# Earlier stream starts, a pause before layer 3, and one transpose for the R rows in a four-layer graph attention kernel

## The chip, the cores and the metric

The kernel runs on one core of one Trainium2 chip. The metric is the device time of one execution in microseconds; the number to beat is the median of three runs.

## What is computed

The input is x of 32 batches, 512 nodes, 256 features, and one 512 x 512 adjacency matrix shared by all batches. Four pre-norm layers follow each other; each adds its output to x. The first three are graph attention layers on relu(layernorm(x)): a projection, two scores per node, a leaky relu of their sum, a softmax over the neighbours, a weighted sum. Layer 2 does this with four heads of 64 features. Layer 3 is a linear layer to 512 features, an attention over all nodes, a linear layer back to 256, and a masked attention.

```python
def _gat(inp, adj_mask, W, a):
    h = jnp.matmul(inp, W)
    f1 = jnp.matmul(h, a[:F_, 0])
    f2 = jnp.matmul(h, a[F_:, 0])
    e = leaky_relu(f1[:, :, None] + f2[:, None, :], ALPHA)
    if adj_mask is not None:
        e = jnp.where(adj_mask[None, :, :] > 0, e, NEG_INF)
    att = jax.nn.softmax(e, axis=2)
    return elu(jnp.einsum('bij,bjf->bif', att, h))
```

## The kernel before

A batch has four tiles of 128 nodes (NT = 4). Everything is float32, so a matmul is two passes on TensorE (15273 records for some 9300 matmuls and transposes); a transpose is one.

**Attention.** exp(leaky_relu(s + r)) is written as a maximum of two products, so the weight of a pair of nodes is max(R of one, T of the other) times the mask. `values` (L301) projects a tile, takes the exponents of the scores on ScalarE (L312, L315) and scales the values (ScalarE L313 in layer 0, VectorE L316 in layer 1; in layer 2, ScalarE L439 and VectorE L440). `weights` (L336) needs R as a row on all 128 partitions. It gets it in one of two ways. Either four broadcast transposes write it into a PSUM bank (L342), or, for heads 1 to 3 of layer 2, it is sent through DRAM: R of all heads is transposed to rows (L460, four transposes of 4 columns), copied to SBUF (L462), written to `row_d` (L464), and read back once per head onto all partitions as `spread` (L468). Then VectorE makes the weights (L346), and `aggregate` (L358) multiplies them with the values.

**Layer 3.** `linear_t` is the first linear layer (tile WM1), `project_half` projects to 512 features in two halves (WFC). For all batches but the last, the unmasked attention is done by sorting (`sort_attend`, L550): indirect DMAs on GpSimd scatter the rows by rank (L594), SP reads them back (L601, L602), VectorE and TensorE make running sums (L612 to L633, tiles `sums` and `tot`), SP writes them to a table (L634, L635), and GpSimd gathers from it (L642). `mlp_in` and a second `linear_t` follow, then the masked attention with WHA, then the store of x (L701).

**Streams and the clock.** Four streams (NS = 4) each work through every fourth batch. A batch is a Python generator that yields the clock value at which its next step may be issued. The loop at the end (L742) always takes the stream with the smallest value, so the order of instructions is set by a clock of the kernel's own, which is arithmetic: `after_us` (L60) adds to the step's own start twice its TensorE cycles over 2400 plus 1.5 times a stated delay. A scheduler below then moves single instructions by a few places. No instruction waits for this clock on the chip; it only orders them. Each engine takes its instructions in the given order. Stream i starts at clock i * LEAD, LEAD = 75; a batch takes 299.4 units, of which layers 0 to 2 take 130.6. The setup of masks and projected weights is a fifth stream from 7.5 on, a step every 4 units. In `turned` (L285) the first half of a layer's input is transposed, then the stream yields `when`, a value handed on from the layer before, and transposes the second half.

**Buffers.** Each stream has two of the eight PSUM banks (`bank`, L74), taken in turn. In SBUF, `w` has 4 buffers, `v` 4, `hT` 3, `xn` 3, `y` and `q` 3 each, `spread` 2, `y4` 1, `x` 5. The SBUF tile for the R rows comes from the `q` pool.

Of the kernel before, what the change touches and what calls it, by code (L numbers as in the profile page):

```python
# [35 lines left out]
def fast(ctx, tc, flag, x, adj, w0, a0, w1, a1, w2, a2, mlp1_w, mlp1_b, mlp2_w, mlp2_b,  # L36
# [10 lines left out]
    LEAD = 75.0  # L47
    SLOW = 1.5
    STRETCH = 2.0

    const = ctx.enter_context(tc.tile_pool(name="const", bufs=1))
    work = ctx.enter_context(tc.tile_pool(name="work", bufs=2))
# [21 lines left out]
    def bank():  # L74
        return psum.tile([P, N], FP, tag=f"b{turn[0]}", name="b", bufs=8 // NS)
# [209 lines left out]
    def turned(xn, when):  # L285

        hT = work.tile([P, KF, N], FP, tag="hT", name="hT", bufs=3)
        turn_pair(xn, hT, 0)
        yield when
        turn_pair(xn, hT, 2)  # L290
        yield after_us(0.6)
        return hT
# [43 lines left out]
    def weights(r_col, t_col, masked=True, r=None):  # L336
# [15 lines left out]
                nc.vector.tensor_scalar(wt[:, j, :], r, t_col(j), None, op0=OP.max)  # L352
        return wt

    def pair(tag="y"):
        return work.tile([P, 2, F], FP, tag=tag, name=tag, bufs=3)

# [6 lines left out]
        nc.vector.reciprocal(r, den)  # L364
        return r

    def plain(hT, w, rs=None):
        v = yield from values(hT, w, rs)
        wt = weights(lambda t: v[:, t, F + 2:F + 3], lambda j: v[:, j, F + 1:F + 2])
        note(v[:, :, F:])  # L370
        yield after_us(3.2)
        return v, wt
# [16 lines left out]
        nc.vector.tensor_tensor(r, q, r, op=OP.add)  # L389

    def layer0(xt, xn, rs, when):
        v, wt = yield from plain((yield from turned(xn, when)), W0)
        xn, rs = new_xn(), small([NT], "rs")
        for t0 in range(0, NT, 2):
            r, q = pair(), pair("q")
            for i in range(2):
                p, rd = averages(v, wt, t0 + i)
                nc.scalar.activation(q[:, i, :], p, AF.Exp, scale=rd)
                nc.scalar.activation(r[:, i, :], p, AF.Relu, scale=rd)
                if i == 0:  # L400
                    yield after_us(0)
            add_elu(xt[:, t0:t0 + 2, :], r, q)
            norm(xt, xn, rs, t0, True)
            last, when = when, after_us(6)
            if t0 == 0:
                yield after_us(0)
        yield last
        return xn, rs, when

    def layer1(xt, xn, rs, when):  # L410
        v, wt = yield from plain((yield from turned(xn, when)), W1, rs)
        xn, rs = new_xn(), small([NT], "rs")
        for t0 in range(0, NT, 2):
            r = pair()
            for i in range(2):
                p, rd = averages(v, wt, t0 + i)
                nc.scalar.activation(r[:, i, :], p, AF.Relu, scale=rd)
                if i == 0:
                    yield after_us(0)
            xr = xt[:, t0:t0 + 2, :]  # L420
            nc.vector.tensor_tensor(xr, xr, r, op=OP.add)  # L421
            norm(xt, xn, rs, t0, True)
            last, when = when, after_us(5)
            if t0 == 0:
                yield after_us(0)
        yield last
        return xn, rs, when

    def layer2(xt, xn, rs, when):
        hT = yield from turned(xn, when)  # L430
        v = work.tile([P, NT, NH, CH], FP, tag="v", name="v2", bufs=4)
        for t in range(NT):
            ps = bank()
            for k in range(KF):
                matmul(
                    ps[:, :NH * CH], hT[:, k, t * P:(t + 1) * P], W2[:, k, :, :], start=(k == 0), stop=(k == KF - 1)
                )
            pv = ps[:, :NH * CH].rearrange("p (h c) -> p h c", c=CH)
            nc.scalar.activation(v[:, t, :, D:], pv[:, :, D:], AF.Exp, scale=rs[:, t:t + 1])  # L439
            nc.vector.scalar_tensor_tensor(  # L440
                v[:, t, :, :D], pv[:, :, :D], rs[:, t:t + 1], v[:, t, :, D:D + 1].to_broadcast([P, NH, D]),
                op0=OP.mult, op1=OP.mult,
            )
            yield after_us(0 if t + 1 < NT else 1)
        ya = work.tile([P, NT, F], FP, tag="y4", name="y4", bufs=1)
        wts = []

        def begin(h):
            wts.append(
                weights(  # L450
                    lambda t: v[:, t, h, D + 2:D + 3], lambda j: v[:, j, h, D + 1:D + 2], r=spread[h] if h else None
                )
            )
            return after_us(3.2)

        p = bank()
        for t in range(NT):
            transpose(p[:NH, t * P:(t + 1) * P], v[:, t, :, D + 2], ident)  # L460
        row = pair("q").rearrange("p a f -> p (a f)")[:NH, :]
        nc.scalar.copy(row, p[:NH, :])  # L462
        row_d = dram.tile([NH, N], FP, tag="row", name="row", bufs=3)
        nc.sync.dma_start(row_d, row)  # L464
        spread = [None]
        for h in range(1, NH):
            r = work.tile([P, N], FP, tag="spread", name="spread", bufs=2)
            nc.sync.dma_start(r, row_d[h, :].partition_broadcast(P))  # L468
            spread.append(r)
        when = begin(0)  # L470
        note(v.rearrange("p t h c -> p (t h) c")[:, :, D:])
        yield after_us(3)
        for h in range(NH):
            last = when
            if h + 1 < NH:
                when = begin(h + 1)
            yield last
            wt = wts[h]
            p = bank()
            for t in range(NT):  # L480
                aggregate(p[:, t * (D + 1):(t + 1) * (D + 1)], wt, t, lambda j: v[:, j, h, :D + 1])
            pv = p[:, :NT * (D + 1)].rearrange("p (t c) -> p t c", c=D + 1)
            r = reciprocal(pv[:, :, D:])
            nc.vector.tensor_tensor(
                ya[:, :, h * D:(h + 1) * D], pv[:, :, :D], r.to_broadcast([P, NT, D]), op=OP.mult
            )
            if h % 2:
                c = slice((h - 1) * D, (h + 1) * D)
                y = ya[:, :, c]
                q = pair("q").rearrange("p a (b f) -> p (a b) f", f=2 * D)  # L490
                nc.scalar.activation(q, y, AF.Exp)
                nc.scalar.activation(y, y, AF.Relu)
                add_elu(xt[:, :, c], y, q)
            yield after_us(0)
        xn, rs = new_xn(), small([NT], "rs")
        for t0 in range(0, NT, 2):
            norm(xt, xn, rs, t0, False)
        yield after_us(7)
        return xn, rs, after_us(2)
# [177 lines left out]
    def layer3(xt, xn, when, b):  # L677
        oT = yield from linear_t((yield from turned(xn, when)), WM1, b1, "oT", 2)
        yield from (attend if b >= B - 1 else sort_attend)(oT, b)
        rT = yield from linear_t(oT, WM2, b2, "rT", 2)  # L680
        v, wt = yield from plain(rT, WHA)
        for t0 in range(0, NT, 2):
            y, q = pair(), pair("q")
            for i in range(2):
                p, rd = averages(v, wt, t0 + i)
                nc.scalar.activation(q[:, i, :], p, AF.Exp, scale=rd)
                nc.scalar.activation(y[:, i, :], p, AF.Relu, scale=rd)
                yield after_us(0)
            elu2_plus1(y, q)
            p = bank()  # L690
            for i in range(2):
                for k in range(KF):
                    transpose(
                        p[:, (i * KF + k) * P:(i * KF + k + 1) * P], rT[:, k, (t0 + i) * P:(t0 + i + 1) * P], ident
                    )
            yf = y.rearrange("p a f -> p (a f)")
            nc.vector.scalar_tensor_tensor(yf, p, -1.0, yf, op0=OP.add, op1=OP.add)  # L697
            nc.scalar.activation(y, y, AF.Relu)  # L698
            xr = xt[:, t0:t0 + 2, :]
            nc.gpsimd.tensor_tensor(xr, xr, y, op=OP.add)  # L700
            nc.sync.dma_start(  # L701
                out[b, t0 * P:(t0 + 2) * P, :].rearrange("(t p) f -> p t f", p=P), xr
            )
            yield after_us(0)
# [12 lines left out]
    def batch(b):  # L717
        xt = xts.pop(b)
        xn, rs = new_xn(), small([NT], "rs")
        for t0 in range(0, NT, 2):  # L720
            norm(xt, xn, rs, t0, False)
        yield after_us(4)
        when = after_us(2)
        for layer in (layer0, layer1, layer2):
            xn, rs, when = yield from layer(xt, xn, rs, when)
        if b + NS < B:
            xts[b + NS] = load_x(b + NS)
        yield from layer3(xt, xn, when, b)


# [4 lines left out]

    ready = {i: i * LEAD for i in range(NS)}
    streams = [stream(i) for i in range(NS)]
    early = setup()  # L740
    ready[NS] = 7.5
# [461 lines left out]
```

## Time and profile before

| what | value |
| --- | --- |
| median of three runs | 2963.7 us (2962.96 to 2964.57) |
| profiled execution: its own time | 2958.47 us |
| its span, first to last instruction | 2956.8 us |
| mean granted clock of TensorE | 0.994 |
| TensorE busy | 2870.2 us |
| VectorE busy | 2270.1 us |
| ScalarE busy | 1493.6 us |
| GpSimd busy | 496.9 us |
| R row transposes, 128 of 4 columns | 19.2 us busy, 272 ns of one |
| copy of the R rows on ScalarE, 32 | 559 ns of one |
| first four batches stored at | 293.3, 382.2, 472.6, 562.2 us |

Durations are those of one profiled execution. The profile counts an engine as busy while any of its instructions runs. TensorE's matmuls are pipelined: one takes longer than the distance to the next, so busy time is no measure of work where matmuls are few. In what follows PE is TensorE, DVE is VectorE, ACT is ScalarE, POOL is GpSimd, SP is the engine that issues most DMAs; L70 is line 70 of the kernel before. L66 and L70 are the helpers through which all matmuls and transposes go, so tiles, not lines, tell them apart.

### The profile page before, as it was taken

To read this page: it belongs to the slowest core of one execution; us is meant where nothing else is said; L and a number is where in the kernel's file an instruction comes from. 1 tells how busy PE (TensorE), PEld (TensorE's weight loads), DVE (VectorE), ACT (ScalarE), POOL (GpSimd) and SP (SyncE) were. 2 spreads that over 40 slices of the span, in tenths; PEclk is the share of its full clock that TensorE was granted. 3 is DMA by queue.
4 is the path that set the end of the run, shared out by engine and by line. 5 is a ranking of instruction groups with operands and counts; after the bars stand their busy time and mean duration, and the time that the engine had idled before them with its cause. 6 is when DMAs were issued, how large, how long until landed. Compare 5 with 4: busy or idle time off the path is not lost.

```text
span 2956.8 us, 43040 instructions
## 1 busy us (share of the span) xinstructions
PE 2870.2 (97%) x15273; PEld 2335.9 (79%) x15273; DVE 2270.1 (77%) x5674; ACT 1493.6 (51%) x3790; POOL 496.9 (17%) x509
## 2 busy tenths in 40 slices
PE   7999999999999999999999999999999999999998
PEld 6777888778888877888778888778878788887765
DVE  4678878778878778878778778788778788787763
ACT  3444455554555544555544555545555544555444
POOL 0011122111122111122011221111221111221120
PEclk9999999999999999999999999999999999999999
DMA  3022233232232332232222232222232222332230
GB/s 93 18 95 94 81 100 115 82 99 98 83 101 96 99 101 89 83 110 96 99 94 87 87 115 92 96 95 88 91 115 90 96 95 81 101 115 73 93 115 16
DMA packets 192765, 270.88 MB, mean 92 GB/s; under 512 B 16992, under 2 KB 155550, under 8 KB 192544
## 3 DMA queue, kind: packets, MB, share of 16 engines
q1 hardware_dynamic: 162784, 169.76, 18.0%
q0 software_dynamic: 29760, 98.30, 9.8%
q8 instruction: 123, 2.02, 0.3%
q14 instruction: 98, 0.80, 0.1%
HBM read 152.62 MB, written 115.39 MB: 91 GB/s over the span
## 4 chain that ended last, share of the span: by engine, by line
PE 85%; DVE 9%; ACT 3%; issue 2%; DMA 1%; POOL 0%; SPq 0%; POOLq 0%; ACTq 0%; DVEq 0%
PE b L66 77%; PE b L70 8%; DVE st L262 2%; DVE xn L273 1%; DVE xn L269 1%; DVE y L697 1%; DVE v L316 1%; ACT rs L265 1%; DVE y L389 0%; DVE w L346 0%; DVE mv L263 0%; DVE x L421 0%; DVE tot L633 0%; ACT q L388 0%; DMA sums<-order 0%
## 5 line engine op out<-in xcount | busy, mean ns | idle before, releaser
L66 PE MATMUL b<-v,w 128*128 128x65 f32 (+1 forms) x7232 | 1218.1, 321 | 9.7 <-DVE w L346 8.2
L66 PEld LDWEIGHTS b<-v,w 128*128 128x128 f32 x7232 | 1052.9, 191 | 164.9 <-issue 40.8
L66 PE MATMUL b<-WFC,oT 128*128 128x256 f32 (+1 forms) x2048 | 499.7, 381 | 3.0 <-ACT ends L515 3.0
L66 PEld LDWEIGHTS b<-WFC,oT 128*128 128x128 f32 x2048 | 374.1, 190 | 51.3 <-ACT v L516 3.6
L66 PE MATMUL b<-W,hT 128*128 128x259 f32 (+1 forms) x1536 | 384.0, 388 | 0.8 <-DVE v L316 0.3
L346 DVE SCALAR_TENSOR_TENSOR w<-b,v,maskT 128x512 f32<-128x512 f32 x512 | 369.8, 743 | 4.9 <-PE b L70 4.9
L594 POOL DMA_INDIRECT order<-v,at x248 | 280.3, 1130 | 467.5 <-DVE w L346 159.8
L66 PEld LDWEIGHTS b<-W,hT 128*128 128x128 f32 x1536 | 285.7, 192 | 47.0 <-ACT hT L283 2.3
L346 DVE SCALAR_TENSOR_TENSOR w<-spread,v,maskT 128x512 f32<-128x512 f32 x384 | 269.4, 741 | 0.5 <-DMA spread<-row 0.5
L364 DVE RECIPROCAL rden<-b 128x1 f32<-128x1 f32 (+1 forms) x516 | 78.1, 163 | 249.4 <-PE b L66 245.1
L700 POOL TENSOR_TENSOR x<-x,y 128x512 f32<-128x512 f32 x64 | 81.6, 1275 | 1100.4 <-ACT y L698 1040.6
L66 PE MATMUL b<-hT,WM 128*128 128x512 f32 x512 | 250.6, 593 | 1.4 <-ACT hT L283 1.4
L642 POOL DMA_INDIRECT g<-table,at x124 | 120.5, 971 | 735.2 <-ACT y L662 373.6
L66 PE MATMUL b<-oT,WM 128*128 128x512 f32 x512 | 231.7, 595 | 0.0
L516 ACT ACTIVATE v<-b,ends 128x256 f32<-128x256 f32 x256 | 119.4, 466 | 183.9 <-PE b L66 179.0
L262 DVE BATCH_NORM_STATS2 st<-x 128x6 f32<-128x256 f32 x512 | 192.6, 407 | 4.8 <-DMA x<-in_x_dram 2.5
L70 PEld LDWEIGHTS b<-ident,xn 128*128 128x128 f32 x1024 | 125.0, 142 | 70.9 <-DVE xn L273 32.9
L389 DVE TENSOR_TENSOR y<-q,y 128x512 f32<-128x512 f32 x192 | 132.6, 691 | 59.9 <-ACT q L388 58.5
L70 PE MATMUL b<-ident,xn 128*128 128x128 f32 x1024 | 155.2, 278 | 21.9 <-DVE xn L273 16.0
L332 ACT ACTIVATE oT<-b,bias 128x512 f32<-128x512 f32 x128 | 88.3, 690 | 169.8 <-PE b L66 169.8
L66 PEld LDWEIGHTS b<-oT,WM 128*128 128x128 f32 x512 | 97.7, 191 | 96.0 <-issue 92.7
L283 ACT ACTIVATE hT<-b 128x512 f32<-128x512 f32 x256 | 146.7, 591 | 46.4 <-PE b L70 46.3
(141 smaller groups left out, 3759.9 us busy)
## 6 DMA issues: line engine op xcount, KB each, us to landing
table<-sums SPq DMA_DIRECT2D x62, 1032.0 KB
sums<-order SPq DMA_DIRECT2D x62, 516.0 KB
spread<-row SPq DMA_DIRECT2D x96, 256.0 KB
x<-in_x_dram SPq DMA_DIRECT2D x32, 512.0 KB
out_dram<-x SPq DMA_DIRECT2D x64, 256.0 KB
sums<-order SPq DMA_DIRECT2D x62, 129.0 KB
order<-v,at POOLq DMA_INDIRECT x248, 2.8
g<-table,at POOLq DMA_INDIRECT x124, 4.4
```

Of the source, the lines that this page charges most:

```text
L66: nc.tensor.matmul(p, w, x, **flags)
L70: instruction = nc.tensor.transpose(p, x, i)
L262: nc.vector.bn_stats(st[:, i, :], xt[:, t0 + i, :])
L283: nc.scalar.activation(hT[:, :, t0 * P:(t0 + 2) * P], p.rearrange("p (k n) -> p k n", k=KF), AF.Relu)
L332: nc.scalar.activation(o[:, f, :], p, AF.Relu, bias=bias[:, f:f + 1])
L346: w = nc.vector.scalar_tensor_tensor(wt[:, j, :], r, t_col(j), maskT[:, j, :], op0=OP.max, op1=OP.mult)
L364: nc.vector.reciprocal(r, den)
L389: nc.vector.tensor_tensor(r, q, r, op=OP.add)
L516: nc.scalar.activation(halves[c][:, t, :F], ps[:, :F], AF.Copy, scale=ends[:, t, 0:1])
L594: nc.gpsimd.indirect_dma_start(out=orders[c], out_offset=bass.IndirectOffsetOnAxis(ap=at[:, 0, t:t + 1], axis=0), in_=halves[c][:, t, :], ...
L642: nc.gpsimd.indirect_dma_start(out=g, out_offset=None, in_=table, in_offset=bass.IndirectOffsetOnAxis(ap=at[:, 1, t:t + 1], axis=0),)
L700: nc.gpsimd.tensor_tensor(xr, xr, y, op=OP.add)
```

## The change

Streams start at clock i * 50 (HEAD) instead of i * 75 (LEAD). Each stream's first batch (b < 4) yields once in front of layer 3, for b * (LEAD - HEAD) units, and its `when` is raised to that value; the x load of the stream's next batch is issued ahead of the pause. The R rows of layer 2 are made by a function of their own, `rows_out`: one transpose of all 16 columns (4 tiles x 4 heads) instead of four of 4, a ScalarE copy of 16 x 128 instead of 4 x 512 into a tile `row` with one buffer of its own, and a DMA that rearranges the 16 rows into the same DRAM layout. `spread` reads a row back as before. `plain` and head 0 of layer 2 could take the way through DRAM too, but the switches for it are off (FAR0 = FAR1 = FARH = 0, HEAD1 = 1): `weights` gets r=None there, as before.

```diff
@@ -47,6 +47,13 @@
     LEAD = 75.0
     SLOW = 1.5
     STRETCH = 2.0
+    HEAD = 50.0
+    SB = 2
+    FAR = 5.0
+    FAR0 = 0
+    FAR1 = 0
+    FARH = 0
+    HEAD1 = 1
 
     const = ctx.enter_context(tc.tile_pool(name="const", bufs=1))
     work = ctx.enter_context(tc.tile_pool(name="work", bufs=2))
@@ -352,6 +359,22 @@
                 nc.vector.tensor_scalar(wt[:, j, :], r, t_col(j), None, op0=OP.max)
         return wt
 
+    def rows_out(cols, n):
+
+        p = bank()
+        transpose(p[:NT * n, :P], cols, ident)
+        row = work.tile([P, P], FP, tag="row", name="row", bufs=1)[:NT * n, :]
+        nc.scalar.copy(row, p[:NT * n, :P])
+        row_d = dram.tile([n, N], FP, tag=f"row{n}", name=f"row{n}", bufs=4)
+        nc.sync.dma_start(row_d.rearrange("n (t p) -> t n p", p=P) if n > 1 else row_d.rearrange("n (t p) -> (n t) p", p=P), row)
+        return row_d
+
+    def spread(row):
+
+        r = work.tile([P, N], FP, tag="spread", name="spread", bufs=SB)
+        nc.sync.dma_start(r, row.partition_broadcast(P))
+        return r
+
     def pair(tag="y"):
         return work.tile([P, 2, F], FP, tag=tag, name=tag, bufs=3)
 
@@ -364,9 +387,13 @@
         nc.vector.reciprocal(r, den)
         return r
 
-    def plain(hT, w, rs=None):
+    def plain(hT, w, rs=None, far=False):
         v = yield from values(hT, w, rs)
-        wt = weights(lambda t: v[:, t, F + 2:F + 3], lambda j: v[:, j, F + 1:F + 2])
+        r = None
+        if far:
+            r = spread(rows_out(v[:, :, F + 2], 1)[0, :])
+            yield after_us(FAR)
+        wt = weights(lambda t: v[:, t, F + 2:F + 3], lambda j: v[:, j, F + 1:F + 2], r=r)
         note(v[:, :, F:])
         yield after_us(3.2)
         return v, wt
@@ -389,7 +416,7 @@
         nc.vector.tensor_tensor(r, q, r, op=OP.add)
 
     def layer0(xt, xn, rs, when):
-        v, wt = yield from plain((yield from turned(xn, when)), W0)
+        v, wt = yield from plain((yield from turned(xn, when)), W0, far=FAR0 > 0)
         xn, rs = new_xn(), small([NT], "rs")
         for t0 in range(0, NT, 2):
             r, q = pair(), pair("q")
@@ -408,7 +435,7 @@
         return xn, rs, when
 
     def layer1(xt, xn, rs, when):
-        v, wt = yield from plain((yield from turned(xn, when)), W1, rs)
+        v, wt = yield from plain((yield from turned(xn, when)), W1, rs, far=FAR1 > 0)
         xn, rs = new_xn(), small([NT], "rs")
         for t0 in range(0, NT, 2):
             r = pair()
@@ -448,25 +475,17 @@
         def begin(h):
             wts.append(
                 weights(
-                    lambda t: v[:, t, h, D + 2:D + 3], lambda j: v[:, j, h, D + 1:D + 2], r=spread[h] if h else None
+                    lambda t: v[:, t, h, D + 2:D + 3], lambda j: v[:, j, h, D + 1:D + 2], r=far[h]
                 )
             )
             return after_us(3.2)
 
 
 
-        p = bank()
-        for t in range(NT):
-            transpose(p[:NH, t * P:(t + 1) * P], v[:, t, :, D + 2], ident)
-        row = pair("q").rearrange("p a f -> p (a f)")[:NH, :]
-        nc.scalar.copy(row, p[:NH, :])
-        row_d = dram.tile([NH, N], FP, tag="row", name="row", bufs=3)
-        nc.sync.dma_start(row_d, row)
-        spread = [None]
-        for h in range(1, NH):
-            r = work.tile([P, N], FP, tag="spread", name="spread", bufs=2)
-            nc.sync.dma_start(r, row_d[h, :].partition_broadcast(P))
-            spread.append(r)
+        row_d = rows_out(v[:, :, :, D + 2], NH)
+        far = [spread(row_d[h, :]) if h >= HEAD1 else None for h in range(NH)]
+        if HEAD1 == 0:
+            yield after_us(FAR)
         when = begin(0)
         note(v.rearrange("p t h c -> p (t h) c")[:, :, D:])
         yield after_us(3)
@@ -678,7 +697,7 @@
         oT = yield from linear_t((yield from turned(xn, when)), WM1, b1, "oT", 2)
         yield from (attend if b >= B - 1 else sort_attend)(oT, b)
         rT = yield from linear_t(oT, WM2, b2, "rT", 2)
-        v, wt = yield from plain(rT, WHA)
+        v, wt = yield from plain(rT, WHA, far=FARH > 0)
         for t0 in range(0, NT, 2):
             y, q = pair(), pair("q")
             for i in range(2):
@@ -725,6 +744,11 @@
             xn, rs, when = yield from layer(xt, xn, rs, when)
         if b + NS < B:
             xts[b + NS] = load_x(b + NS)
+        if b < NS:
+
+            pause = begun[0] + b * (LEAD - HEAD)
+            yield pause
+            when = max(when, pause)
         yield from layer3(xt, xn, when, b)
 
 
@@ -735,7 +759,7 @@
 
 
 
-    ready = {i: i * LEAD for i in range(NS)}
+    ready = {i: i * HEAD for i in range(NS)}
     streams = [stream(i) for i in range(NS)]
     early = setup()
     ready[NS] = 7.5
```

## Prediction

> **What bounds the kernel now.** I read the page's busy table first, then its chain that ended last, then busy time by stage, then the waits of the tensor engine in one steady stretch, then the timeline around them.
>
> ```profile
> span 2956.8 us, 43040 instructions
> ...
> PE 2870.2 (97%) x15273; PEld 2335.9 (79%) x15273; DVE 2270.1 (77%) x5674; ACT 1493.6 (51%) x3790; POOL 496.9 (17%) x509
> ...
> PE 85%; DVE 9%; ACT 3%; issue 2%; DMA 1%; POOL 0%; SPq 0%; POOLq 0%; ACTq 0%; DVEq 0%
> ```
>
> TensorE is busy 97% of the span and carries 85% of the chain. So a cycle of PE work removed is time removed, and otherwise only PE idle time can be won: 2956.8 - 2870.2 = 86.6 us. Where it lies shows in windows cut where the layer 3 of batches 0, 1, 2, 3, 4 and 5 begins (first `b<-hT,WM` matmul of each). Columns: stretch, length, busy PE, weight load, VectorE, ScalarE, GpSimd, granted clock, DMA share, GB/s.
>
> ```profile
> 0.00:111.10 111.10, 90.32 (x489) 73.81 (x489) 64.49 (x190) 39.13 (x106) 4.10 (x10) 0.94 0.24 70
> 111.10:186.30 75.20, 70.01 (x375) 57.55 (x375) 46.53 (x128) 30.84 (x83) 9.97 (x10) 0.95 0.14 43
> 186.30:267.40 81.10, 80.03 (x433) 65.30 (x434) 64.04 (x164) 40.96 (x106) 13.01 (x14) 1.00 0.29 92
> 267.40:356.30 88.90, 87.75 (x475) 72.06 (x474) 71.40 (x178) 46.49 (x118) 15.54 (x16) 1.00 0.30 96
> ...
> 1071.00:1428.00 357.00, 351.56 (x1888) 287.64 (x1886) 283.53 (x708) 185.28 (x472) 63.20 (x64) 1.00 0.29 96
> ```
>
> The steady state does four batches in 357 us with 5.4 us of PE idle. The fill (first two windows) idles 20.8 + 5.2 us at a lower clock. The rest is the drain. But busy time flatters the fill, since a lone matmul is shown longer than its share of a full pipeline. I therefore price PE work by cadence, which timeline rows of merged matmuls give (start, length, engine, line, tiles, how many):
>
> ```profile
> 1160.47 1.02 PE L66 MATMUL b<-hT,WM 128*128 128x512 f32 x2
> ...
> 1196.31 2.62 PE L66 MATMUL b<-W,hT 128*128 128x268 f32 x11
> ...
> 1198.76 1.89 PE L66 MATMUL b<-WFC,oT 128*128 128x256 f32 x8
> ...
> 1201.80 1.04 PE L70 MATMUL b<-ident,v 128*4 128x128 f32 x8
> ...
> 1210.84 1.17 PE L66 MATMUL b<-v,w 128*128 128x65 f32 x9
> ```
>
> Taking off the last one's own duration and dividing by the others: (1.04 - 0.27) / 7 = 0.11 us for a transpose, (1.89 - 0.38) / 7 = 0.216 for a pass of 256 columns, (2.62 - 0.39) / 10 = 0.223 for 268, (1.17 - 0.27) / 8 = 0.112 for 65, 1.02 - 0.59 = 0.43 for 512; a matmul call is two passes. Medians over the steady state agree (0.109, 0.215, 0.226, 0.112, 0.429). Counted so, the four fill windows hold 71.8, 66.2, 79.6 and 87.5 us of work, and lose 39.3, 9.0, 1.5 and 1.4; a steady batch holds 87.7 in 89.3.
>
> [...] the trace has 272 ns for the 4-row ones, but their cadence is 0.11 us, and that is what a removed one is worth. [...] the first two windows show 0.94 and 0.95, all later ones 1.00. [...] here the queue waited 60.5 us in 32 times (1.9 us) for `row` to land. [...]
>
> **The change, part by part.**
>
> *R rows by one transpose.* Four transposes of 4 columns become one of 16: 3 x 32 = 96 less, x 0.109 = 10.5 us of PE work. Less if the engine would have waited there anyway: the single transpose needs the last tile's exp, while three of the old four did not. Bounds: 0 to 14.4 us (96 x 0.15, the busy share of each); I take 10.5. The ScalarE copy shrinks from 4x512 (0.56 us) to 16x128; ScalarE is 51% busy, so 0. The `row` tile has one buffer: a copy must wait for the previous batch's write, 1.9 us, and copies are at least 67 us apart now (some 40 in the new fill): 0. The q pool loses a user: 0 or a small gain, no q wait on a row DMA is listed. The write in 64 pieces of 512 B instead of 4: between 0 and 1 us later, an estimate from its 1.9 us; the readers waited 0.5 us for `spread` in total, so 0. If that cover is gone, the first reader, VectorE's w of head 1, holds the VectorE queue up to 1 us a batch, 32 us. The other new switches (FAR0, FAR1, FARH at 0, HEAD1 at 1) choose the old path: 0.
>
> *The earlier starts and the pause.* The clock is arithmetic in the code, so it can be worked out without a chip. Layer 3 of stream 0 begins at 130.6 units before and 129.9 after; streams 1 to 3 are 50 apart, then pause 25, 50, 75 units, and so begin layer 3 at 204.9, 279.9, 354.9 (before 205.6, 280.6, 355.6). Everything after the fill keeps its order in the main; only the first four batches' layers 0 to 2 move earlier. Work per stretch of clock (to 130, 205, 280, 355), summed with the cadences: 88.0, 86.0, 70.3, 60.4 us after, against 71.8, 66.2, 79.6, 87.5: 36 us are pulled forward and paid back by thinner stretches. First stretch: until clock 50 nothing changes (48 us); the rest took 63 us for 46.6 of work and now has 62.7; with 6 us lost (bounds 2 and 10) 69, so 117 in all, against 111.1. Second: 86.0 plus 2.5 lost = 88.5, against 75.2. Third and fourth: the loss by number of running streams is 9.0 at 2.67 on average (second window before) and 1.5 at 3.67 (third), so 4.0 at 3.33 and 6.5 at 3: 74.3 and 66.9, against 81.1 and 88.9. Sum 346.7 against 356.3: -9.6. If the loss goes by the work in a stretch instead, 6.7 and 12 are lost there, and the sum is 355: -1. I take the middle, -5.5, less 1.3 that R's part already counts: -4.5.
> Moved along are each early batch's row write and three spreads on SP: batch 2's now stand ahead of batch 0's table stores, and batch 3's ahead of batch 1's sums reads. SP waits in order, so a row write waiting for its copy holds those sorts' DMAs; the sort's own distance on PE is 27 us or more of other work, so 0, at worst the 3.1 us that PE waited once for `tot` in the fill. GpSimd has nothing in layers 0 to 2. All x loads of batches 0 to 3 stay first.
>
> *The pause's side effect on all later batches.* A paused stream takes `when = pause`, and so skips the 3 units between the halves of `turned`; streams 1 to 3 stay 3 units early. Gaps are 72, 75, 75, 76.7 instead of 75, 75, 75, 74.4, and 28 batches interleave differently. The waits of PE in the steady stretch from 1071 to 1428 us are few (total, times, longest; then one of them in the timeline, with the idle time in brackets):
>
> ```profile
> PE b L70 <- DVE v L316: 4.3, 5, 0.9
> PE b L70 <- DVE xn L273: 2.2, 4, 0.8
> ...
> 1159.98 0.41 PEld L70 LDWEIGHTS b<-ident,v 128*128 128x128 f32 x4 [1.11 <-DVE v L316]
> ```
>
> In each batch, layer 1's R transposes wait about 1.0 us (start to start 1.03) for VectorE to empty their bank, after 0.87 us of other streams' work: they need 1.9. In the new program order the four streams have 4.8, 1.7, 0.4 and 1.3 us there: waits of 0, 0.2, 1.5, 0.6, so 2.3 for 4.1 in four batches. In turn layer 2's, which had 3.05 us or more and never waited, have 0.4, 1.3, 1.3, 3.05; they need ScalarE's 0.27 and VectorE's 0.49 plus queueing, 1.1 to 1.9: 0.7 to 2.7 in four batches, I take 1.5. Layer 0's first xn transposes keep about 2.8. Other covers that the order shows thinned: +1 (0 to 4). Sum 2.3 + 1.5 + 2.8 + 1 = 7.6 against 4.1 + 2.8 = 6.9: +0.7 in four batches, x 7 = +5, less 3 where the removed R transposes would only have waited: I take +2. Behind such a wait on PE every stream's matmuls are queued, so it counts in full.
>
> Sum: -10.5 - 4.5 + 2 = -13 us. The profiled run took 2958.47 us (span 2956.8 and 1.7 around it), 5.2 below the median of 2963.7; the difference is put on the median: 2950.7, rounded 2951.
>
> **Rivals.** (1) As summed: 2951, own range 2943 to 2957.5; chance 0.55. For it: the PE-bound chain. (2) The pause gives all back and covers thin a little more: -10.5 + 0 + 6.5 = -4, 2960 (2958 to 2969); chance 0.2. For it: the fourth stretch's 60 us of work; against: only three streams run there. (3) The thin stretches run as fast as a lone stream does (batch 0 reaches layer 2's first transposes, clock 77, at 62.8 us: 0.82 us a unit, 62 a stretch) or as their work lets them: 62 for the fourth and 70.3 + 1.5 for the third, 339.3 in all, -17; with R and the steady waits -10.5 - 15.7 + 2 = -24, 2939.5 (2934 to 2943); chance 0.11. For it: the first window before keeps nearly that pace with few streams; against: the second loses 9 us with 2.67. (4) Slower: the new interleave uncovers layer 2's R transposes (after `rows_out`) in all streams, 1.9 us each without layer 1's relief: 1.9 - 0.8 covered = 1.1 a batch, x 28 = +31, less the 15 gained: 2980. It decides from (15 + 6) / 28 = 0.75 us of new wait a batch. For it: 0.4 us of cover in stream 0; against: 3.05 in stream 3. Chance 0.14. That the single transpose doesn't save PE cadence is in (2).
>
> **How the numbers follow.** About 0.2%, 5.9 us, is what a measurement of this kernel can tell from no change: faster is below 2957.8, slower above 2969.6. Faster is (1) and (3), 0.66; same (2), 0.2; slower (4), 0.14. The range, 2934 to 2967, leaves out (4) and a few hundredths at the ends of (2) and (3).
>
> **What would show it.** Right: 32 transposes of 16 columns in the place of 128 of 4, cadence kept; layer 3 of batch 3 begins near 347 us instead of 356.3; steady four batches near 356.7 us (357.3 before, - 1.3 + 0.7). Wrong: fourth stretch at 73 us or more; a new line of PE waiting for VectorE's L440 evictions, or VectorE waiting for `spread`; four batches above 358.

## The result and the profile after

| what | before | after |
| --- | --- | --- |
| median of nine runs each | 2962.16 us (2959.9 to 2964.74) | 2972.24 us (2969.46 to 2977.08) |
| ratio, 95% interval | | 1.0033, 1.0023 to 1.0042 |
| span of the profiled execution | 2956.8 us | 2970.9 us |

The change makes the kernel about 10 us slower: the forecast has the wrong sign, and its range missed the time. The spans differ by 14.1 us because the profiled execution of before (2958.47 us) lay 3.7 below its median. Line numbers of the kernel after are higher by 7 up to the weights and by 19 in the sort (before's L273, L283, L316, L346, L628 are L280, L290, L323, L353, L647).

The page of the kernel after: span, busy time, chain that ended last.

```profile
span 2970.9 us, 42835 instructions
...
PE 2886.7 (97%) x15177; PEld 2329.9 (78%) x15177; DVE 2257.7 (76%) x5674; ACT 1494.7 (50%) x3790; POOL 496.2 (17%) x509
...
PE 74%; DVE 14%; ACT 5%; DMA 4%; issue 2%; POOL 0%; SPq 0%; POOLq 0%; DVEq 0%; ACTq 0%
```

TensorE does 96 instructions less and yet shows 16.5 us more busy time: a trap, since the profile shows a matmul at its full length (383 ns on average for 257 columns), all of which counts when it runs alone, while in a full pipeline it adds only its cadence (218 ns). The chain says more: VectorE's share went from 9 to 14%, ScalarE's from 3 to 5%, DMA's from 1 to 4%. The windows, cut as before at the layer 3 starts of batches 0 to 4, with one steady stretch of four batches last:

```profile
0.00:120.40 120.40, 104.69 (x579) 88.49 (x580) 77.45 (x233) 47.93 (x133) 4.09 (x10) 0.96 0.22 64
120.40:200.20 79.80, 75.68 (x420) 63.59 (x418) 54.40 (x149) 35.88 (x100) 8.56 (x10) 0.98 0.13 42
200.20:260.30 60.10, 59.27 (x308) 49.21 (x308) 44.98 (x110) 23.76 (x60) 6.26 (x8) 0.91 0.25 84
260.30:353.70 93.40, 86.96 (x415) 63.04 (x415) 65.56 (x154) 44.58 (x106) 22.81 (x23) 0.96 0.38 116
...
1075.00:1433.60 358.60, 353.60 (x1877) 286.73 (x1876) 281.63 (x709) 185.61 (x472) 63.22 (x64) 1.00 0.30 95
```

Layer 3 of batch 3 begins at 353.7 us, 2.6 earlier than before instead of the 9 forecast, and four steady batches take 358.6 us in this stretch (358.3 to 360.6 from one layer 3 start of a stream to its next) instead of 357.4. After 32 batches the gap is 14.1 us.

Busy time doesn't tell where it went, so I counted *lost* time: the time elapsed minus all TensorE records begun so far, each at its cadence (0.109 us a transpose, 0.112, 0.218, 0.226 and 0.429 a pass of 65, 256, 268 and 512 columns). Lost up to a moment, in us, with two experiments (e1: the R part alone; e3: R part and early start, with the old distances between streams):

| up to | 100 | 175 | 225 | 300 | 350 | 450 | 2800 | 450 to 2800 |
| --- | --- | --- | --- | --- | --- | --- | --- | --- |
| before | 32.1 | 41.3 | 47.5 | 48.9 | 48.7 | 51.3 | 101.2 | 49.9 |
| e1 | 32.5 | 41.4 | 46.9 | 48.2 | 48.1 | 50.9 | 102.5 | 51.6 |
| e3 | 26.2 | 27.6 | 37.1 | 38.7 | 51.0 | 53.4 | 104.4 | 51.0 |
| after | 27.8 | 28.8 | 40.4 | 47.5 | 54.9 | 57.7 | 125.3 | 67.6 |

Against before, the early start wins 12.5 us by 175 us and has given back 18.7 by 350: the fill is 6.4 worse at 450. Of these 6.4, e3 shows only 2.1; the other 4.3 came with the new distances. The steady state loses 17.7 more. The R part takes out 10.5 us of work. 6.4 + 17.7 - 10.5 = 13.6, of the 14.1.

**Where the steady state loses.** What TensorE waited for between 540 and 2690 us (24 batches; total, times, longest), before:

```profile
PE b L70 <- DVE v L316: 20.6, 24, 1.0
PE b L70 <- DVE xn L273: 13.0, 24, 0.8
```

and after:

```profile
PE b L77 <- DVE xn L280: 10.6, 24, 0.8
PE b L73 <- ACT hT L290: 8.2, 12, 0.7
PE b L77 <- DVE v L323: 4.2, 6, 0.7
PE b L73 <- DVE sums L638: 2.9, 5, 0.6
PE b L77 <- DVE y L416: 1.4, 6, 0.2
```

The wait for `v` fell from 20.6 to 4.2, as forecast. New is ScalarE's `hT`, 8.2 us, and a tail of small ones. The list alone would still mislead: with its five lines not shown here it sums to 30.5 us, *less* than the 33.6 before. It counts only time in which no matmul was in flight. Start-to-start distance minus cadence counts the draining too (us per four batches, same window):

| place where TensorE waits | forecast | before | after |
| --- | --- | --- | --- |
| layer 1's R transposes, for VectorE's `v` | 2.3 | 4.3 | 1.0 |
| head of layer 3: second xn pair, first WM1 matmul | not seen | 0 | 3.2 |
| layer 0's first xn pair | 2.8 | 3.4 | 2.3 |
| layer 2's R transposes | 1.5 | 0 | no line of PE waiting for it |
| all else | 1 | -0.1 | 3.7 |
| sum | 7.6 | 7.5 | 10.2 |

The first two rows together hardly changed: 4.3 and 4.2. The wait at layer 1 wasn't removed, it moved. The timeline of after at the head of a layer 3 (start, length; in brackets the idle time before):

```profile
1165.79 0.95 DVE L647 TENSOR_TENSOR sums<-sums,b 128x774 f32<-128x774 f32 x1
...
1166.66 0.73 DVE L280 TENSOR_SCALAR xn<-x,mv,rs 128x256 f32<-128x256 f32 x2
...
1167.12 0.87 PE L77 MATMUL b<-ident,xn 128*128 128x128 f32 x4 [0.22 <-DVE xn L280]
...
1168.03 0.60 ACT L290 ACTIVATE hT<-b 128x512 f32<-128x512 f32 x1 [0.50 <-PE b L77]
...
1168.68 0.70 PE L73 MATMUL b<-hT,WM 128*128 128x512 f32 x1 [0.69 <-ACT hT L290]
```

and of e3, which keeps the old order at this place:

```profile
1156.20 1.04 PE L77 MATMUL b<-ident,xn 128*128 128x128 f32 x8
...
1156.84 1.08 ACT L290 ACTIVATE hT<-b 128x512 f32<-128x512 f32 x2 [0.17 <-PE b L77]
...
1158.11 0.65 PE L77 MATMUL b<-ident,v 128*128 128x128 f32 x4 [0.87 <-DVE v L323]
...
1158.60 0.59 PE L73 MATMUL b<-hT,WM 128*128 128x512 f32 x1
```

In e3 all eight xn transposes go through at once, and while TensorE stands 0.87 us for one stream's `v`, ScalarE finishes the other stream's `hT`: the WM1 matmul then waits for nothing. One wait covers two needs. In after, the sort's 0.95 us addition (L647) comes ahead of the second xn pair in VectorE's order, so the xn and `hT` waits stand bare.

**Where the fill gives back.** The timeline of after (SPq is SP's DMA queue):

```profile
194.61 0.55 SPq L620 DMA_DIRECT2D sums<-order  x1
...
195.94 0.43 DVE L633 TENSOR_TENSOR sums<-sums 128x258 f32<-128x258 f32 x1 [4.25 <-DMA sums<-order]
...
196.74 1.40 DVE L353 SCALAR_TENSOR_TENSOR w<-b,v,maskT 128x512 f32<-128x512 f32 x2
...
197.54 0.50 PE L73 MATMUL b<-v,w 128*128 128x65 f32 x2 [3.42 <-DVE w L353]
```

VectorE stands 4.25 us for batch 0's sort rows; batch 2's `w`, whose transposes had ended at 192.51 us, is behind that in its order, and TensorE stands 3.42 us for it. I had looked for such a meeting on SP's queue, and costed it at nothing, at worst 3.1 us; this one is in VectorE's order.

What came after the wait cost more than the wait. The granted clock in the 13.6 us behind it, and a group of passes there whose cadence is otherwise 0.112 us:

```profile
197.80:211.40 13.60, 13.23 (x49) 11.25 (x49) 9.05 (x19) 1.50 (x4) 0.00 (x0) 0.50 0.21 73
...
202.10 5.65 PE L73 MATMUL b<-v,w 128*128 128x65 f32 x26
```

The clock was half, and a pass took 5.65 / 26 = 0.22 us. At half clock 13.6 us lose up to 6.8 us of work, twice the wait; the two together are most of the 11.6 us lost between 175 and 225 us. Up to 450 us all stretches at half clock add up to 30.7 us in after and 20.5 in before, so up to 15.4 and 10.2 us are lost to them: the clock can hold up to 5.2 of the 6.4 by which the fill is worse. Over all executions the median of the mean granted clock was 0.992 for after and, in the e, f and g runs, 0.994 for before; 0.002 of the time is 5.9 us. From 450 to 2800 us the clock was 1.00 in both, so the steady loss is not the clock's.

Later, between 300 and 350 us, with stream 3 paused, 7.4 us are lost in after (54.9 - 47.5) and 12.3 in e3, against none before: three streams don't fill TensorE there.

### The profile page after: what moved, and what is told of

It reads as the page before. It is cut to its first block, busy times and chain, and to the rows that moved or that the text cites. A ratio compares the mean times of both kernels' runs of the same rounds, so it can differ in the third digit from the quotient of the medians.

```text
span 2970.9 us, 42835 instructions
## 1 busy us (share of the span) xinstructions
PE 2886.7 (97%) x15177; PEld 2329.9 (78%) x15177; DVE 2257.7 (76%) x5674; ACT 1494.7 (50%) x3790; POOL 496.2 (17%) x509
## 4 chain that ended last, share of the span: by engine, by line
PE 74%; DVE 14%; ACT 5%; DMA 4%; issue 2%; POOL 0%; SPq 0%; POOLq 0%; DVEq 0%; ACTq 0%
PE b L73 66%; PE b L77 7%; DVE st L269 2%; DMA order<-v,at 2%; DVE w L353 1%; DMA sums<-order 1%; DVE xn L280 1%; DVE y L416 1%; DVE x L410 1%; DVE sums L647 1%; DVE y L409 1%; DVE v L323 1%; ACT hT L290 1%; DVE junk L592 1%; DVE xn L276 1%
## 5 line engine op out<-in xcount | busy, mean ns | idle before, releaser
L73 PE MATMUL b<-v,w 128*128 128x65 f32 (+1 forms) x7232 | 1224.0, 321 | 13.6 <-DVE w L353 10.0
L73 PEld LDWEIGHTS b<-v,w 128*128 128x128 f32 x7232 | 1063.8, 192 | 200.3 <-issue 62.9
L73 PE MATMUL b<-W,hT 128*128 128x259 f32 (+1 forms) x1536 | 392.7, 389 | 3.6 <-DVE y L716 1.5
L353 DVE SCALAR_TENSOR_TENSOR w<-b,v,maskT 128x512 f32<-128x512 f32 x512 | 366.2, 744 | 2.5 <-PE b L77 1.9
L353 DVE SCALAR_TENSOR_TENSOR w<-spread,v,maskT 128x512 f32<-128x512 f32 x384 | 272.8, 741 | 4.6 <-DMA spread<-row 4.6
L290 ACT ACTIVATE hT<-b 128x512 f32<-128x512 f32 x256 | 150.4, 594 | 105.0 <-PE b L77 104.1
L77 PE MATMUL b<-ident,xn 128*128 128x128 f32 x1024 | 162.3, 278 | 15.1 <-DVE xn L280 12.1
```

What stands on the lines that cost most here:

```text
L73: nc.tensor.matmul(p, w, x, **flags)
L77: instruction = nc.tensor.transpose(p, x, i)
L290: nc.scalar.activation(hT[:, :, t0 * P:(t0 + 2) * P], p.rearrange("p (k n) -> p k n", k=KF), AF.Relu)
L353: w = nc.vector.scalar_tensor_tensor(wt[:, j, :], r, t_col(j), maskT[:, j, :], op0=OP.max, op1=OP.mult)
```

## The experiments

Medians of 4 to 21 executions, with the ratio to before as run on the same chip (before: 2961.14 us for the e runs, 2961.28 for f, 2962.62 for g).

**Taking the change apart.** The theory after the result: the R part gains, and the loss is in the new distances between streams (72, 75, 75, 76.7 units instead of 75, 75, 75, 74.4). Rivals: the fill carries the loss; or the single transpose does.

*e1: the R part alone.* The old clock is kept by adding the three removed transposes to the clock's count, without issuing them.

```diff
-    HEAD = 50.0
+    HEAD = 75.0
...
         transpose(p[:NT * n, :P], cols, ident)
+        spent[0] += (NT - 1) * 2 * P
```

> R rows by one transpose alone: streams 75 units apart, no pause, and the kernel's clock charged as for four transposes, so that the order of all other instructions stays that of before. Theory A (three separate parts: R saves 10.5 us, the earlier start with its pause costs about 6, the shifted stream distances cost about 18 over the rest): 2962 - 10.5 = 2951.5 us. Theory B (the new way of making R brings the small waits itself, through its single wait for all four tiles and its longer DMA): 2966 us or more.

Measured: 2947.09 us, 0.9951 (0.9938 to 0.9965): 14 us faster than before, the best version here that computes everything, and better than both kernels. Its order on TensorE agrees with before's in some 98% of places, its waits are before's. The single transpose isn't to blame.

*e2: the new distances alone, with the R part, no early start.*

```diff
-        if b < NS:
-
-            pause = begun[0] + b * (LEAD - HEAD)
-            yield pause
-            when = max(when, pause)
...
-    ready = {i: i * HEAD for i in range(NS)}
+    ready = {i: i * LEAD - (3.0 if i else 0.0) for i in range(NS)}
```

> R by one transpose, streams starting at 0, 72, 147, 222 units without pause: the distances that the changed kernel has after its pause, so its order from the second batch of each stream on, but the fill of before. Theory A: 2972 less the 6 us that early start and pause cost, 2966. Theory C (the fill is what costs, and carries into the rest): below 2955.

Measured: 2977.34 us, 1.0057 (1.0043 to 1.007), 30 us above e1 without any early start. 8.0 of it is lost by 450 us (58.9 against 50.9; at most 5.2 of these by the half clock), most of the rest in the steady state, where its waits have after's pattern.

*e3: R part and early start, old distances.* A paused stream's `when` lies 3 units past its pause, and e1's line is kept.

```diff
         transpose(p[:NT * n, :P], cols, ident)
+        spent[0] += (NT - 1) * 2 * P
...
-            when = max(when, pause)
+            when = max(when, pause + 2 * SLOW)
```

> The changed kernel with the 3 units given back that a paused stream skips, and the clock charged as for four transposes: early start and pause as in the change, but afterwards the order of before. Theory A: 2951.5 plus 6 for the fill, 2957.5. Theory C (the fill carries into the rest): 2970 or more. Theory B: 2970 or more.

Measured: 2950.85 us, 0.9964 (0.9951 to 0.9978). So the early start by itself costs 3.8 us (e3 against e1; the two sets of five executions barely overlap, 2948.71 to 2951.78 and 2945.04 to 2949.01): its fill gain is given back whole. The median granted clock fell with it, from 0.995 to 0.993, at most 5.9 us of the time, so the clock can hold all of the 3.8; no run separates it. And the same early start with the new distances costs some 20 more by the ratios (after against e3). The distances hold the loss, the early start a small part.

*e4: the change with four transposes of 4 columns again*, on the change's own clock, with the old copy and write.

```diff
-        transpose(p[:NT * n, :P], cols, ident)
-        row = work.tile([P, P], FP, tag="row", name="row", bufs=1)[:NT * n, :]
-        nc.scalar.copy(row, p[:NT * n, :P])
+        for t in range(NT):
+            transpose(p[:n, t * P:(t + 1) * P], cols[:, t, :], ident)
+        spent[0] -= (NT - 1) * 2 * P
+        row = pair("q").rearrange("p a f -> p (a f)")[:n, :]
+        nc.scalar.copy(row, p[:n, :])
...
-        nc.sync.dma_start(row_d.rearrange("n (t p) -> t n p", p=P) if n > 1 else row_d.rearrange("n (t p) -> (n t) p", p=P), row)
+        nc.sync.dma_start(row_d, row)
```

> The changed kernel with the R rows made by four transposes into a tile of the q pool as before, the clock charged as for one, so that the order of all else stays that of the changed kernel. Theory A: 2972 + 10.5 = 2982.5. Theory B: 2962 to 2968, since the new waits go with the single transpose.

Measured: 2979.28 us, 1.0061 (1.0047 to 1.0075). The R part is worth 7 to 8 us here and 14 in e1; the 10.5 lies between. Its steady waits are after's (10.1 us per four batches).

**How little a shift it takes.** The single transpose also takes 0.64 units off each batch's clock, which makes the last distance 73.7 instead of 74.4.

*f1: the R part on its own clock*, the change with only the early start undone.

```diff
-    HEAD = 50.0
+    HEAD = 75.0
```

> R rows by one transpose alone, streams 75 apart, no pause, the clock charged as the change charges it (256 cycles for the one transpose): distances 75, 75, 75 and 73.7 units. Theory D (the steady loss depends on where each stream stands against the next, and the distances of 72 and 76.7 are a bad case, while a unit less in one distance is not): 2945 to 2953. Theory E (any departure from even distances of 75 uncovers new waits): 2958 or more.

Measured: 2956.09 us, 0.9982 (0.9975 to 0.9988): 9 us above e1, for 0.64 units. It fell between the two expectations.

*g4: the change with its 3 units given back.*

```diff
-            when = max(when, pause)
+            when = max(when, pause + 2 * SLOW)
```

> The changed kernel with one edit, the 3 units that a paused stream skips given back; the clock charged as the change does: distances 75, 75, 75, 73.7. If early start and clock charge add up: 2947 + 4 + 9 = 2960; if only the 72 and 76.7 matter: 2951.

Measured: 2961.40 us, 1.0 (0.9991 to 1.0008). This completes a staircase, each step with the ratios' differences times 2962 us: R work -14.5 (e1), early start +3.8 (e3), R's 0.64 units off the clock +10.7 (g4), 3 units off the first distance +9.8 (after). They sum to the change's +9.8 because each step starts where the last one ended; the test is f1, which prices the third step without the early start at +9.2 (0.9982 against 0.9951). From the intervals of the ratios each step is uncertain by some 4 to 6 us.

*f3: e3 with starts 65 apart.*

```diff
-    HEAD = 50.0
+    HEAD = 65.0
```

> As early start with the old order afterwards, but streams 65 instead of 50 units apart, with pauses of 10, 20 and 30 units. Theory F (what the early start wins by full use of the first 175 us the pause gives back, in proportion): between 2947.1 (no early start) and 2950.9 (50 units): 2947 to 2951. Theory G (the giving back comes only when the pause leaves fewer than three streams' work; a short pause costs nothing): 2941 or less.

Measured: 2963.31 us, 1.0005 (0.9997 to 1.0014): worse than 50 and than 75, against both expectations. Its profiled execution (2968.06 us) is its slowest. By 125 us that has lost some 17 us more than e3, counted as above. The first part of it, in the timeline:

```profile
90.06 0.45 PE L77 MATMUL b<-ident,xn 128*128 128x128 f32 x1 [2.20 <-ACT rs L272]
...
91.80 6.93 PE L73 MATMUL b<-v,w 128*128 128x65 f32 x32
```

and 32 such passes at the same place in e3, at full clock:

```profile
86.01 3.68 PE L73 MATMUL b<-v,w 128*128 128x65 f32 x32
```

TensorE waits 2.20 us for a layer norm, and then its granted clock is 0.50 from 90.0 to 110.4 us; the passes take 6.93 us instead of 3.68. That stretch alone loses up to 10.2 us. Up to 450 us the stretches at half clock add up to 54.6 us in f3 and 27.3 in e3: up to 13.6 of the 15 us by which f3's fill is worse. Over all executions the median granted clock is 0.990 in f3 and 0.993 in e3. A smaller part is a meeting on VectorE:

```profile
112.55 0.75 DVE L353 SCALAR_TENSOR_TENSOR w<-b,v,maskT 128x512 f32<-128x512 f32 x1
113.22 0.74 DVE L269 BATCH_NORM_STATS2 st<-x 128x6 f32<-128x256 f32 x2
...
115.52 0.70 PE L73 MATMUL b<-v,w 128*128 128x257 f32 x2 [1.46 <-DVE w L353]
```

One stream's weights and another's layer norm fall on VectorE together, and TensorE waits for weights twice within 2.2 us (1.52 and 1.46). Whether an early start pays is a matter of what meets what, and of what the clock does after it.

*g3: e3 with the 72 in the second place* (75, 72, 75, 77.4).

```diff
-            when = max(when, pause + 2 * SLOW)
+            when = max(when, pause + (2 * SLOW if b == 1 else 0))
```

> Early start and pause, clock charged as for four transposes, the 3 units given back to stream 1 alone: distances 75, 72, 75 and 77.4. Theory J (a stream waits at the head of its layer 3 when the next one follows at another distance than 75, since layer 1's R transposes of the next then miss the place behind it): the waits stand in streams 1 and 3, where the change has them in 0 and 3, and the time is near the changed kernel's 2972, 2965 to 2978. Theory K (streams 0 and 3 are special, by their banks or tables): waits in 3 alone and 2950 to 2962.

Measured: 2984.99 us, 1.008 (1.0066 to 1.0094), the slowest of these. The head of layer 3 waits 3.5 us per four batches, 2.65 of it in stream 0 (after: 1.5 in stream 0 and 1.6 in stream 3), layer 1's R transposes 0, all else 6.6. Neither theory named these places; the wait again moved from layer 1 to layer 3.

**What stands ahead in VectorE's order.** If L647, 0.95 us, is what makes the waits, they should shrink without it.

*f5 and f6: the addition on GpSimd*, in the change (f5) and in e1 (f6). It reads ScalarE's copy of the totals in SBUF instead of the PSUM bank.

```diff
-            nc.vector.tensor_tensor(
-                sums[:, 1:, 0, :], sums[:, 1:, 0, :], pv[:, None, :C].to_broadcast([P, NT - 1, C]), op=OP.add
+            nc.gpsimd.tensor_tensor(
+                sums[:, 1:, 0, :], sums[:, 1:, 0, :], sums[:, 0:1, 0, :].to_broadcast([P, NT - 1, C]), op=OP.add
```

> The changed kernel with the addition of the running totals to the sums (128 x 774, 0.95 us, twice a batch) taken from VectorE to GpSimd. Theory H (around the start of a layer 3 VectorE's order sets PE's waits: the second xn pair and the bank eviction of layer 1 stand behind this addition): the 3.3 us of layer 3's waits in four batches go, and some others: 2972 - 20 = 2952. Theory I (those waits come from the order of PE alone): 2970 to 2974. If GpSimd's scatters and gathers get late behind the additions: 2980 or more.

> R alone in the order of before, with the same addition on GpSimd. Theory H: layer 1's R transposes wait less than the 4.1 us in four batches, 2947 - 15 to 20 = 2930. Theory I: 2945 to 2949. If GpSimd gets late: 2955 or more.

Measured: 3019.98 us, 1.02 (1.0186 to 1.0214), and 2989.45 us, 1.0091 (1.0076 to 1.0107). Both slower, so this took the cost off VectorE only in name. The timeline of f6:

```profile
1165.58 1.83 POOL L648 TENSOR_TENSOR sums<-sums 128x774 f32<-128x774 f32 x1 [19.10 <-ACT sums L647]
1165.99 1.56 DVE L280 TENSOR_SCALAR xn<-x,mv,rs 128x256 f32<-128x256 f32 x1
```

This L280, 0.41 us elsewhere, takes 1.56 and ends 0.14 us after GpSimd's addition. Waits rose to 17.3 us per four batches in f5 and 12.8 in f6. The runs change two things at once, where the addition is done and how fast VectorE does its own work beside it, and settle nothing on L647.

*g1 and g2: the addition left out*, in the change (g1) and in e1 (g2). The sorted attention then lacks its running totals, so only the time is of use.

```diff
-            nc.vector.tensor_tensor(
-                sums[:, 1:, 0, :], sums[:, 1:, 0, :], pv[:, None, :C].to_broadcast([P, NT - 1, C]), op=OP.add
-            )
```

> The changed kernel without the addition of the running totals to the sums (VectorE, 128 x 774, 0.95 us, twice a batch): the sorted attention of layer 3 is then wrong, so this measures time alone. Theory H2 (VectorE's order around the head of a layer 3 sets PE's waits there; on GpSimd the same addition slowed VectorE's neighbours and so lengthened them): the waits at layer 3's head fall from 3.2 us in four batches to under 1.5, and the time by 10 us or more: 2962 or less. Theory I (the order of PE alone sets them): the waits stay, 2969 to 2973.

> R alone in the order of before, with the same addition left out (time alone). Theory H2: layer 1's R transposes wait less than 4.3 us in four batches, 2937 or less. Theory I: 2945 to 2948.

Measured: g1 2962.40 us, 0.9998 (0.9989 to 1.0006), and g2 2938.48 us, 0.9924 (0.9911 to 0.9938): by the ratios 10 below after and 8 below e1. The waits of TensorE in g2 from 1071 to 1426 us:

```profile
PE b L77 <- DVE xn L280: 2.2, 4, 0.8
PE b L73 <- ACT hT L290: 0.6, 4, 0.2
```

The four waits of 0.9 us for `v` are gone (in the sum by start to start 4.3 to 1.0), and at once a small `hT` wait shows that they had covered (0 to 1.65 at the head of layer 3). In g1 the head of layer 3 falls from 3.2 to 1.5, but all else rises from 3.7 to 5.5, and the sum only from 10.2 to 9.7; of g1's 10 us some 3 lie between 450 and 2800 us, the rest in fill and drain. So VectorE's lateness at these places is shown, and that L647 is about half of it at the head of layer 3; that L647 explains the slowdown is not, since the two versions stay 22 us apart (by their ratios) without it.

## Why the prediction was wrong, point by point

- **R rows by one transpose: -10.5, right.** By time it is 14 in the old order and 7 to 8 in the change's. The cadence cost of these transposes fell from 1.74 to 0.45 us per four batches, 1.3 saved as summed, times 8. The copy takes 250 ns and hides. The group of after (busy us, mean ns; then idle time before it) against 128 of 272 ns before, and the write on SP (least, median, most ns):

```profile
L77 PE MATMUL b<-ident,v 128*16 128x128 f32 x32 | 8.8, 275 | 0.4 <-ACT v L466 0.4
```

```profile
L369 SPq DMA_DIRECT2D row<-row x32: 628/677/726, 79.9 to 2821.7; - x32
```

- **The write costed at 0 to 1 us later, cover intact: nearly.** VectorE waited 4.6 us for `spread` in four times, against 0.5 in one; e1, with the same write, is 14 us faster than before, so it isn't what decides. The prediction miscounted the pieces: 8 KB in pieces of 512 B are 16, not 64. SP's queue waited 1.3 us on average for `row` to land (39.0 us in 31 times), where before it had waited 1.9 (60.5 in 32).
- **Fill: -4.5, wrong; +6.4.** The mechanism was right in shape: work was pulled forward and paid back. The gain was 12.5, not 17 (48.3 lost in the first two stretches before, 31.5 forecast). Paid back were 18.7; the two ways to sum it gave 8 and 16. Three terms failed: the meeting of streams costed at 0 (3.4 us of TensorE's idle time at 197 us); the clock, which the prediction shows at 0.94 and 0.95 in the old fill, but which has no term in its sum (up to 5.2 us more lost at half clock than before); and the loss with three running streams, taken as 6.5 in a whole stretch: 7.4 went within 50 us. The sum has a slip too: the middle of -9.6 and -1 is -5.3, and less 1.3 that is -4.0, not -4.5.
- **The pause's side effect: +2, the step that failed; about +18.** The prediction said "waits of 0, 0.2, 1.5, 0.6, so 2.3 for 4.1". The relief came, even more of it (1.0). What failed is that it was booked as a gain. In the old order that wait also hid the `hT` eviction and the next stream's xn; without it 3.2 us appeared at the head of layer 3. The term "Other covers that the order shows thinned: +1 (0 to 4)" measured 7 with that place, 3.7 without. Layer 2's R transposes, my feared place, show no listed wait. Per four batches +2.7 instead of +0.7, and nothing of the 3 taken off. The distances that do this hold two shifts, the pause's 3 units and the 0.64 that the R part takes off the clock; by the staircase they cost 9.8 and 10.7, fill included.
- **Rivals (2) and (3).** (2) let the pause give all of the early start back, and e3 shows that (+3.8), but it put 6.5 on the pause's side effect. (3) let the fourth stretch run at a lone stream's pace, 62 us; it took 93.4.
- **Rival (4), slower:** the sign was its own, the place was not. Its deciding point, 0.75 us of new wait a batch, was worked out against a fill that gains 4.5. Measured: 2.7 / 4 = 0.68 a batch, but with a fill that loses 6.4, so that only 4.1 of the R part's 10.5 was left to use up. That the sign came out was luck.
- **What would show it wrong** did: fourth stretch 93.4 us (bound 73), four batches 358.6 (bound 358), VectorE waiting for `spread`.

Open: what in the order sets each of the small waits in "all else" (the largest: the sort's sums +0.7, W2's values, the transposes of `y` and layer 2's aggregates for `w` some +0.6 each per four batches); how much of the fill's loss is the clock's, for which only upper bounds are worked out here; and why starts 50, 65 and 75 apart give +3.8, +16 and 0: only the meetings and the slow stretches named above are shown. A shift of the distances other than by 0.64 and 3 units wasn't tried.

## What to carry to other kernels

When an engine that takes its instructions in a given order is late for several customers, a wait removed at one of them can come out at the next, as it did here (4.3 to 1.0 us at layer 1, 0 to 3.2 at the head of layer 3): before booking the gain, ask what else was finished under that wait. In a kernel whose order comes from a clock of its own, an edit that shortens the clock is two edits; keep the clock (e1) to see the edit's own worth. A listing of idle time on a pipelined engine can fall while the loss grows (33.6 to 30.5 us here, while the loss per four batches went from 7.5 to 10.2); count start to start against the cadence. And look at the granted clock behind a wait of a few microseconds: here 13.6 us at half clock, which lose up to 6.8 us of work, came behind a wait of 3.42.

## What the runs showed of the hardware that was not expected

- VectorE ran slower beside GpSimd: with the addition on GpSimd (1878 ns on average, against 955 on VectorE), VectorE's L280 rose from 409 to 539 ns on average, with single ones up to 1565, and its L639 from 480 to 655 (f6 against e1). In the trace of f6 above, the slowed L280 starts while GpSimd's addition runs and ends 0.14 us after it. By what means the one holds up the other, no run shows.
- Issuing the row write took SP 677 ns in 16 pieces by 512 B, against 273 in 4 rows by 2048 B (medians; the page of after counts 512 more packets under 2 KB, 16 for each of the 32 writes).
- The granted clock fell again to 0.91 and 0.96 in the two stretches around the pause, where before it had stayed at 1.00. In the fill it was full or half, and the stretches at half clock were multiples of 3.41 us: 13.65 behind a wait of 3.42 us in after, 20.48 behind one of only 2.20 us in f3. What sets the clock down, and for how long, no run shows.
